# Moving start-up loads, position writes and scale rows between DMA queues, and one image's projections in the stage order, in a fused two-block convolution kernel

## The chip, the cores and the metric

The kernel runs on one core of a Trainium2 chip. Its time is the device time of one execution in microseconds (us); 18 executions of the kernel before were measured. One more thing about names: TensorE multiplies matrices (PE in the profile), VectorE (DVE) and ScalarE (ACT) work element by element, GpSimd (POOL) fills constants here and issues DMAs, SyncE (SP) only issues DMAs. Each engine runs its own instructions strictly in order, so a DMA that an engine issues also waits for what stands ahead of it on that engine.

## What is computed

Two bottleneck blocks, one after the other, on 16 images of 1024 channels and 32x32 pixels, all in float32. Cut to what matters, with `bn` a scale and a shift per channel:

```python
# block 0: 1x1 convolution to 256 channels, 3x3 self-attention, 1x1 convolution back
h = relu(bn(conv1x1(x, w_conv1)))
q, k, v = relu(bn(conv1x1(h, wq))), relu(bn(conv1x1(h, wk))), bn(conv1x1(h, wv))
logit[tap] = sum over 8 channels of a head of q * (k shifted by tap + pos[tap])   # 9 taps
a = relu(bn(sum over taps of softmax(logit)[tap] * (v shifted by tap)))
x = relu(bn(conv1x1(a, w_conv3)) + x)
# block 1: 1x1, 3x3 and 1x1 convolutions; inv = gamma / sqrt(var + eps)
y = relu(bn(conv1x1(x, w1)))
y = relu(bn(conv3x3(y, w2)))
x = relu(bn(conv1x1(y, w3)) + x)
```

## The kernel before, in words

**Stages.** The work on TensorE is a list of stages written out by hand (lines 933 to 938), one letter and an image number each. `C` is the first convolution of an image (`first_conv`: 8 chunks of 128 channels, each loaded as a 512 KB tile `x`), `Q` the projections to k, q and the position term, `V` the projection to v; `P` stands for C, Q and V in a row. `F` (`fused`) is the end of block 0 together with the first convolution of block 1, in 8 chunks that need `x` again as `s` and write their sum to DRAM as `r`. `W` (`winograd_conv`) is the 3x3 convolution for four images at once in Winograd form: 18 products, each with a transformed weight piece `U` and a transformed input piece `V__`. `U` (`last_sum`) is the last convolution: 8 chunks that load `r` back, seed the sum with it, and write to `out_dram`. A chunk of 8 matrix products takes 3.43 us.

**Side work.** The attention of an image (`logits`, `weighted`) and the Winograd transform of an image (`transform`, 22 us) run on VectorE beside the stages. The class `Side` keeps a model of both engines' time with fixed costs and decides by it in which order VectorE's steps are put into the program; the order is fixed when the program is built. `side.finish(b)` puts all of an image's attention ahead of its stage F.

**Buffers and queues.** `xpool` has 8 tiles; `more_loads` (line 304) issues the next load whenever a tile was given up, in the order of the list `loads`, from GpSimd (from ScalarE for image 0). `wpool` has 6 weight tiles, loaded from SyncE by `more_weights` in the order of use; a weight is loaded anew when its last use is more than 3 stages back. `zpool` has 3 tiles, shared by the softmax trees, the transforms, the Winograd sums and the scale rows. A transform writes its pieces to DRAM (`v<-v`, line 690) in three pairs of columns, (1, 2), (3, 4) and (0, 5); a `V__` load of part 0 or 1 reads columns of the first two pairs and a load of part 2 the last pair. In the kernel before, every `V__` load of four images stands behind all three pairs of the last image (`forms`, lines 310 and 694).

**DMA slots.** The compiled program shows that the DMAs issued by SyncE and ScalarE share 8 completion semaphores in turn, and those issued by GpSimd have 8 of their own: a DMA is issued only when the one eight places earlier, by the same group, has landed.

**Start.** `at_first` (line 1115) sets the order. ScalarE first takes the square root of the norms (line 151, behind a load of its function table), then issues four `x` tiles, three taps `g` (the 3x3 weights, 384 KB each, line 248), three `x`, three taps, the last `x`, and the last convolutions' weights (line 211, four tiles of 512 KB). SyncE loads the first convolution's weights in eight pieces (line 126), then `wqk` and `wv` (line 128), then the scale rows (`scale_rows`, line 221): 1024 scales of a norm stand in SBUF as 128 partitions x 8 and are written to DRAM transposed, `o p -> p o`, so each 4-byte element goes to its own address; the row is then read back to all partitions (line 223). VectorE works out the norms (lines 150 to 160) and the position table (183, 189), then transforms the 3x3 weights from the taps (`winograd_weights`, lines 259 to 281).

**In a stage Q.** `q` is written to DRAM from SyncE (line 490) to be read back in another layout by GpSimd (line 520). The position term (line 470) is copied by ScalarE out of PSUM into the place of q's first half (line 479), which therefore waits until that half of q has been written to DRAM; ScalarE then issues two writes `pos<-q` (line 484).

**At the end of a chunk.** `Expand.result` (line 396) adds the shift and clips on ScalarE (1.1 us for 128x1024) and stores the tile from GpSimd.

Of the kernel before, what the change touches and what calls it, by code (L numbers as in the profile page):

```python
# [8 lines left out]
F32 = mybir.dt.float32  # L9
AF = mybir.ActivationFunctionType  # L10
# [61 lines left out]
def sa_bottleneck_kernel(ctx: ExitStack, tc: tile.TileContext, x, w1t, wqkvt, w3t, u1t, u2t, u3t, params, out):  # L72
# [38 lines left out]
    def more_weights():  # L111

        if not queue:
            return
        key = name, of, half = queue.pop(0)
        t = wpool.tile([P, HW], F32, tag="w", name=f"{name}{half}_{of[0]}")
        src = source(name, half)
        n, k = src.shape[-1], 1
        for d in src.shape[1:-1]:
            k *= d  # L120
        view = t[:, : k * n].rearrange("p (c n) -> p c n", n=n)
        if len(src.shape) == 4:
            view = t.rearrange("p (m j o) -> p m j o", m=NW, j=2)
        if of[1] == 0 and name == "w1":
            for c in range(k):
                nc.sync.dma_start(view[:, c], src[:, c])
        else:
            nc.sync.dma_start(view, src)
        pieces[key] = view
# [17 lines left out]
    bn_a = const.tile([P, _NBN], F32, tag="bn_a", name="bn_a")  # L147
    bn_r = const.tile([P, _NBN], F32, tag="bn_r", name="bn_r")
    bn_t = const.tile([P, _NBN], F32, tag="bn_t", name="bn_t")
    nc.vector.tensor_scalar(bn_a, bn_block("L1_conv_v1"), EPS, None, ALU.add)  # L150
    nc.scalar.activation(bn_r, bn_a, AF.Sqrt)

    nc.vector.reciprocal(bn_t, bn_r)
    nc.vector.tensor_mul(bn_t, bn_t, bn_a)
    nc.vector.tensor_add(bn_t, bn_t, bn_r)
    nc.vector.tensor_scalar(bn_t, bn_t, 0.5, None, ALU.mult)
    nc.vector.reciprocal(bn_r, bn_t)
    nc.vector.tensor_mul(bn_inv, bn_r, bn_block("L1_conv_g1"))
    nc.vector.tensor_mul(bn_t, bn_inv, bn_block("L1_conv_m1"))
    nc.vector.tensor_sub(bn_sh, bn_block("L1_conv_b1"), bn_t)  # L160


    members = const.tile([P, G], F32, tag="members", name="members")
# [17 lines left out]
    for n in range(NW):  # L181
        for half, name in enumerate(("L0_conv_pos_h", "L0_conv_pos_w")):
            nc.vector.tensor_tensor(
                offsets[:, n, 2 * half : 2 * half + 2],
                col(name, 3 * n, 2),
                col(name, 3 * n + 2).to_broadcast([P, 2]),
                ALU.subtract,
            )
        nc.vector.tensor_tensor(
            pos[:, n],  # L190
            members.unsqueeze(2).to_broadcast([P, G, NPOS]),
            offsets[:, n].unsqueeze(1).to_broadcast([P, G, NPOS]),
            ALU.mult,
        )

# [9 lines left out]
    def load_scaled():  # L205

        rooms = vh.rearrange("p r w -> p (r w)"), hpool.tile([P, 2 * HW], F32, tag="h", name="scaled")
        for which, src in enumerate((w3t, u3t)):
            for half in range(2):
                at = rooms[which][:, half * HW :][:, :HW].rearrange("p (n o) -> p n o", n=NW)  # L210
                nc.scalar.dma_start(at, src.rearrange("(n p) o -> p n o", p=P)[:, :, halves(half)])
                scaled[which, half] = at

    def clear_hidden():
# [2 lines left out]
    def scale_rows():  # L217

        for which, scale in enumerate((col("L0_conv_bn3_s", 0, NC), bn_inv[:, 2 * NW : 2 * NW + NC])):
            row = dram.tile([NC, P], F32, tag=f"row{which}", name="row")  # L220
            nc.sync.dma_start(row.rearrange("o p -> p o"), scale)
            t = zpool.tile([P, HW], F32, tag="z", name="scales")
            nc.sync.dma_start(t, AP(row.tensor, row.offset, [[0, P], [1, C]]))
            scales.append(t)

    def scale_weights():

        for which in range(2):
            for half in range(2):
                t = scaled[which, half]  # L230
                nc.vector.tensor_tensor(
                    t, t, scales[which][:, halves(half)].unsqueeze(1).to_broadcast([P, NW, HALF]), ALU.mult
                )
                nc.sync.dma_start(ws[which, half], t)
                yield 1.3


# [3 lines left out]
    def load_taps(m):  # L241
        n = 3 * WID

        tag, shape = (("e", [P, KK, JPIX]), ("bnv", [P, HEAD_DIM, HALO]))[m]
        t = apool.tile(shape, F32, tag=tag, name="g").rearrange("p a b -> p (a b)")
        g = [t[:, i * n : (i + 1) * n] for i in range(3)]
        for i in range(3):
            nc.scalar.dma_start(g[i], u2t[m * P : (m + 1) * P, i * n : (i + 1) * n])
        taps.append(g)

    def winograd_weights():
# [53 lines left out]
    def more_loads():  # L305

        while credits[0] and loads:
            kind, b, c = loads[0]
            if kind == "V":
                if forms.get(b, 0) < NK:  # L310
                    return
                src = form_room(b)[c[0], c[1]].rearrange("p k j e -> p (k j e)")
            elif kind == "r":
                if (b, c) not in stored:
                    return
                src = stored[b, c]
# [5 lines left out]
            (nc.scalar if kind == "x" and b == 0 else nc.gpsimd).dma_start(t, src)  # L322
            loaded[loads.pop(0)] = t
            credits[0] -= 1
# [34 lines left out]
    class Expand:  # L359
# [28 lines left out]
        def result(self, o, to):  # L388
            t = self.tiles.pop(o)
            ps, to_ = self.ahead.pop(o), t  # L390

            if self.kind == "s":
                ps, to_ = ps.rearrange("p (n j) -> p j n", j=4), t.rearrange("p (j n) -> p j n", j=4)
            else:
                ps, to_ = ps.rearrange("p (j n) -> p n j", j=4), t.rearrange("p (n j) -> p n j", j=4)
            nc.scalar.activation(to_, ps, RELU, bias=self.shift(o), scale=1.0)  # L396
            nc.gpsimd.dma_start(to, t)  # L397
            return t
# [23 lines left out]
    def project(b):  # L422
# [42 lines left out]
        def positions():  # L465

            ps = psum.tile([P, HW], F32, tag="ps", name="ps")
            for half in range(2):
                for n in range(NW):
                    nc.tensor.matmul(  # L470
                        ps[n * G * NPOS : (n + 1) * G * NPOS, halves(half)],
                        pos[:, n].rearrange("p g t -> p (g t)"),
                        q[:, n, halves(half)],
                        start=True,
                        stop=True,
                    )

            by_offset = q[:, 0, :]
            nc.scalar.activation(by_offset, ps, AF.Identity)

            room, backs["pos"] = by_quarter("pos", b, JPIX, NPOS)
            by_offset = by_offset.rearrange("p (j w) -> p j w", j=NJ)
            for n in range(NW):
                nc.scalar.dma_start(room[n], by_offset[n * G * NPOS : (n + 1) * G * NPOS])

        k = halo("bnk", 1, RELU)
        yield next(k)
        for n in range(NW):
# [160 lines left out]
    def transform(b, src):  # L649
# [47 lines left out]
        more_loads()  # L697

    def winograd_conv(b):

# [215 lines left out]
    stages = []  # L916
    for text in (
# [4 lines left out]
    ):  # L922
# [190 lines left out]
    made = []  # L1113

    def at_first():
        credits[0] = 4
        more_loads()
        load_taps(0)
        credits[0] = 3
        more_loads()  # L1120
        load_taps(1)
        credits[0] = CHUNKS - 7
        more_loads()
        load_scaled()
# [4 lines left out]
        scale_rows()  # L1129
        hooks["conv1", 2, 0] = clear_hidden  # L1130

    at_first()
# [42 lines left out]
```

## Time and profile before

| | us |
|---|---|
| median of 18 executions | 2476.07 (2468.81 to 2482.71) |
| the profiled execution, its own time | 2475.61 |
| span of its instructions | 2473.7 |
| TensorE busy with products | 2399.3 |
| VectorE busy | 2076.6 |
| ScalarE busy | 918.2 |
| GpSimd busy | 411.0 |
| first product starts | 10.61 |
| last product ends | 2467.47 |
| data moved by DMA | 709.94 MB, 287 GB/s in the mean |

How to read it: "busy" counts the time in which an engine executes, and issuing a DMA counts for GpSimd alone. The time outside the span (1.9 us here) lies ahead of the first instruction and behind the last. A wait is listed with the event that ended it. The DMA queue q10 is ScalarE's, q1 is SyncE's and q0 is GpSimd's; all three run on the same 16 DMA engines. The granted clock of TensorE in a stretch is 1.00 at full speed.

### The profile page before, as it was taken

The numbers are of one execution on the slowest core, as the hardware profiler recorded it, in microseconds if no ns is written. First come the engines' busy times: TensorE is split into PE (matmuls) and PEld (weight loads), VectorE is DVE, ScalarE is ACT, GpSimd is POOL, SyncE is SP. The second block draws the span as 40 slices with busy tenths as digits, with TensorE's granted clock in tenths as the row PEclk, the third lists the DMA queues.
The fourth block names the chain that finished last, engine by engine and source line by source line (L and its number), as shares of the span: only waits on it lengthen the run. The fifth ranks groups of instructions, "written<-read, shape, count | busy, mean of one in ns | idle before, by whom it ended". The sixth has DMA issues, their size and how long they took to land.

```text
span 2473.7 us, 18390 instructions
## 1 busy us (share of the span) xinstructions
PE 2399.3 (97%) x6144; PEld 1157.1 (47%) x6144; DVE 2076.6 (84%) x1631; ACT 918.2 (37%) x873; POOL 411.0 (17%) x777
## 2 busy tenths in 40 slices
PE   5999999999999999999999999999999999998998
PEld 2444444444457443444457443444466444434843
DVE  2799998989989999998889999799989999964700
ACT  1423232242312574324222564324222553343275
POOL 1110101011111122111111122111111121112122
PEclk8999999999999999999999999999999999999999
DMA  8977787877888899788789899689788797789888
GB/s 257 352 260 268 251 286 241 268 238 266 304 288 267 306 332 330 264 295 298 247 263 322 306 310 349 237 296 314 259 306 300 275 354 251 280 307 306 300 248 279
DMA packets 328429, 709.94 MB, mean 287 GB/s; under 512 B 22672, under 2 KB 201872, under 8 KB 319632
## 3 DMA queue, kind: packets, MB, share of 16 engines
q0 software_dynamic: 110592, 441.24, 50.3%
q1 hardware_dynamic: 205792, 250.45, 31.3%
q10 hardware_dynamic: 11952, 17.09, 2.3%
q8 instruction: 49, 0.80, 0.1%
q14 instruction: 44, 0.36, 0.0%
HBM read 433.67 MB, written 275.03 MB: 286 GB/s over the span
## 4 chain that ended last, share of the span: by engine, by line
PE 73%; DMA 13%; issue 7%; DVE 4%; POOL 2%; ACT 1%; ACTq 0%; SPq 0%; POOLq 0%; DVEq 0%
PE ps L346 31%; PE ps L377 22%; PE ps L432 12%; PE ps L723 8%; DMA out_dram<-r 6%; DMA q<-q 1%; PE ps L470 1%; DMA row<-bn_inv 1%; DVE acc L590 1%; POOL r L322 1%; DVE acc L603 1%; DMA U<-uw 1%; DMA s<-in_x_dram 1%; DMA row<-par 1%; ACT h L975 1%
## 5 line engine op out<-in xcount | busy, mean ns | idle before, releaser
L377 PE MATMUL ps<-a,w 128*128 128x512 f32 x1024 | 464.9, 599 | 10.9 <-ACT ps L370 6.0
L346 PE MATMUL ps<-x,w 128*128 128x512 f32 x1024 | 449.9, 601 | 25.4 <-DMA x<-in_x_dram 25.4
L346 PE MATMUL ps<-s,u 128*128 128x512 f32 x1024 | 458.1, 593 | 1.0 <-ACT s L396 1.0
L377 PE MATMUL ps<-y,u 128*128 128x512 f32 x1024 | 442.4, 593 | 7.5 <-ACT ps L370 7.5
L539 DVE TENSOR_TENSOR prod<-qc,bnk 128x2048 f32<-128x2048 f32 x144 | 324.1, 2287 | 8.0 <-DMA a<-acc 6.3
L590 DVE TENSOR_TENSOR acc<-e,bnv 128x2048 f32<-128x2048 f32 x144 | 327.5, 2283 | 3.6
L346 PEld LDWEIGHTS ps<-x,w 128*128 128x128 f32 x1024 | 197.4, 193 | 274.7 <-issue 255.0
L377 PEld LDWEIGHTS ps<-a,w 128*128 128x128 f32 x1024 | 195.7, 192 | 262.4 <-issue 240.1
L396 ACT ACTIVATE s<-ps,par 128x1024 f32<-128x1024 f32 x128 | 142.4, 1113 | 464.5 <-PE ps L377 387.0
L377 PEld LDWEIGHTS ps<-y,u 128*128 128x128 f32 x1024 | 194.3, 190 | 253.6 <-issue 236.4
L346 PEld LDWEIGHTS ps<-s,u 128*128 128x128 f32 x1024 | 194.9, 190 | 245.8 <-issue 237.3
L603 DVE TENSOR_TENSOR acc<-acc 128x2048 f32<-128x2048 f32 x128 | 293.4, 2292 | 4.4
L432 PE MATMUL ps<-h,wqk 128*128 128x512 f32 x512 | 228.7, 602 | 8.5 <-ACT h L975 8.5
L397 POOL DMA_DIRECT2D r<-s x128 | 68.3, 533 | 730.2 <-ACT s L396 713.6
L396 ACT ACTIVATE r<-ps,bn_sh 128x1024 f32<-128x1024 f32 x128 | 141.8, 1108 | 110.5 <-PE ps L377 106.8
L544 DVE TENSOR_TENSOR prod<-prod 128x2048 f32<-128x2048 f32 (+1 forms) x80 | 166.2, 2077 | 2.3
L432 PEld LDWEIGHTS ps<-h,wqk 128*128 128x128 f32 x512 | 97.4, 192 | 137.3 <-issue 111.7
L370 ACT ACTIVATE ps<-r 128x1024 f32<-128x1024 f32 x128 | 130.3, 1020 | 50.9 <-DMA r<-r 37.9
L975 ACT ACTIVATE h<-ps,par 128x1024 f32<-128x1024 f32 x32 | 38.4, 1203 | 287.1 <-PE ps L346 287.1
L370 ACT ACTIVATE ps<-s 128x1024 f32<-128x1024 f32 x128 | 131.1, 1024 | 22.7 <-DMA s<-in_x_dram 19.0
L444 ACT ACTIVATE kp<-ps,par 128x1024 f32<-128x1024 f32 x64 | 77.2, 1207 | 133.6 <-PE ps L432 123.6
L322 POOL DMA_DIRECT2D s<-in_x_dram x128 | 67.8, 530 | 301.4 <-PE ps L346 186.8
(307 smaller groups left out, 2238.1 us busy)
## 6 DMA issues: line engine op xcount, KB each, us to landing
s<-in_x_dram POOLq DMA_DIRECT2D x128, 512.0 KB, 6.4
r<-s POOLq DMA_DIRECT2D x128, 512.0 KB, 4.9
r<-r POOLq DMA_DIRECT2D x128, 512.0 KB, 5.8
out_dram<-r POOLq DMA_DIRECT2D x128, 512.0 KB, 6.5
x<-in_x_dram POOLq DMA_DIRECT2D x120, 512.0 KB, 5.6
v<-v SPq DMA_DIRECT2D x96, 408.0 KB, 5.1
U<-uw SPq DMA_DIRECT2D x72, 512.0 KB, 7.3
bnk<-kp SPq DMA_DIRECT2D x32, 680.0 KB, 7.3
```

The lines of the kernel that those rows point to most:

```text
L322: (nc.scalar if kind == "x" and b == 0 else nc.gpsimd).dma_start(t, src)
L346: nc.tensor.matmul(ps[n][:, halves(half)], wt[:, c % (NC // 2), n * P : (n + 1) * P], src[:, halves(half)], start=(c == 0), stop=(c == NC ...
L370: nc.scalar.activation(ps, t, AF.Identity)
L377: nc.tensor.matmul(self.ahead[o][:, halves(half)], pieces[key][:, n, o % (NC // 2) * P :][:, :P], self.src[:, n, halves(half)], start=Fals ...
L396: nc.scalar.activation(to_, ps, RELU, bias=self.shift(o), scale=1.0)
L432: nc.tensor.matmul(ps[:, halves(half)], pieces[key][:, m, at : at + P], h[:, m, halves(half)], start=(m == 0), stop=(m == NW - 1),)
L444: nc.scalar.activation(dst, src, func, bias=col(f"L0_conv_{name}_b", n), scale=col(f"L0_conv_{name}_s", n),)
L539: nc.vector.tensor_tensor(by_row(t[:, two]), by_row(qc), kc[:, :, i : i + JROWS, j : j + W], ALU.mult)
L544: nc.vector.tensor_add(u[:, :, 0:4], u[:, :, 0:4], u[:, :, 4:8])
L590: nc.vector.tensor_tensor(by_row(dst), rows(e[:, k, :]).unsqueeze(1).to_broadcast([P, HEAD_DIM, JROWS, W]), vc[:, :, i : i + JROWS, j : j ...
L603: nc.vector.tensor_add(acc, acc, t)
L723: nc.tensor.matmul(acc[i][:, at, :, n, :], pieces[key][:, m, at, n * P : (n + 1) * P], v[:, at, :, m * (TILES + TR) :][:, :, :TILES], star ...
```

## The change

- At the start, ScalarE issues all eight `x` tiles of image 0 first; the square root and VectorE's norms come behind them (`norms()`), the position table later still (`position_table()`). Taps and last weights are issued by GpSimd. The first convolution's first weight half comes in two pieces (one channel block, then three) and the second half in one.
- The scale rows are written as they stand, 128 partitions x 8 elements (32 bytes in a row), and read back, by GpSimd; the multiplication of the last weights reads the scales in the new order (`p (m o) -> p o m`).
- `q` and the position term are written to DRAM by GpSimd. The position term is copied into a tile of `zpool` of its own.
- `V__` loads of parts 0 and 1 may be issued when the pairs (1, 2) and (3, 4) of the fourth image are on their way, those of part 2 when its pair (0, 5) is.
- The stage P10 moves from between F5 and F6 to behind F7, directly ahead of C11. P10 and C11, Q11 then share their `w1` and `wqk` loads.
- The very last output chunk is clipped in two halves, by ScalarE and VectorE, and stored in two halves by ScalarE's and SyncE's queues.

```diff
-            for c in range(k):
-                nc.sync.dma_start(view[:, c], src[:, c])
+            for part in (slice(0, 1), slice(1, k)) if half == 0 else (slice(0, k),):
+                nc.sync.dma_start(view[:, part], src[:, part])
...
-    nc.vector.tensor_scalar(bn_a, bn_block("L1_conv_v1"), EPS, None, ALU.add)
-    nc.scalar.activation(bn_r, bn_a, AF.Sqrt)
+    def norms():
+        nc.vector.tensor_scalar(bn_a, bn_block("L1_conv_v1"), EPS, None, ALU.add)
+        nc.scalar.activation(bn_r, bn_a, AF.Sqrt)
...
-                nc.scalar.dma_start(at, src.rearrange("(n p) o -> p n o", p=P)[:, :, halves(half)])
+                nc.gpsimd.dma_start(at, src.rearrange("(n p) o -> p n o", p=P)[:, :, halves(half)])
...
-            row = dram.tile([NC, P], F32, tag=f"row{which}", name="row")
-            nc.sync.dma_start(row.rearrange("o p -> p o"), scale)
+            row = dram.tile([P, NC], F32, tag=f"row{which}", name="row")
+            nc.gpsimd.dma_start(row, scale)
             t = zpool.tile([P, HW], F32, tag="z", name="scales")
-            nc.sync.dma_start(t, AP(row.tensor, row.offset, [[0, P], [1, C]]))
+            nc.gpsimd.dma_start(t, AP(row.tensor, row.offset, [[0, P], [1, C]]))
...
-            nc.scalar.dma_start(g[i], u2t[m * P : (m + 1) * P, i * n : (i + 1) * n])
+            nc.gpsimd.dma_start(g[i], u2t[m * P : (m + 1) * P, i * n : (i + 1) * n])
...
-                if forms.get(b, 0) < NK:
+                if forms.get((b, c[1] == 2), 0) < NK:
...
+            if (self.kind, self.b, o) == ("r", B - 1, NC - 1):
+                one, two = slice(0, JPIX // 2), slice(JPIX // 2, JPIX)
+                nc.scalar.activation(to_[:, one], ps[:, one], RELU, bias=self.shift(o), scale=1.0)
+                nc.vector.tensor_scalar(to_[:, two], ps[:, two], self.shift(o), 0.0, ALU.add, ALU.max)
+                nc.scalar.dma_start(to[:, :HALF], t[:, :HALF])
+                nc.sync.dma_start(to[:, HALF:], t[:, HALF:])
+                return t
...
-            by_offset = q[:, 0, :]
+            by_offset = zpool.tile([P, HW], F32, tag="z", name="by_offset")
...
-                nc.scalar.dma_start(room[n], by_offset[n * G * NPOS : (n + 1) * G * NPOS])
+                nc.gpsimd.dma_start(room[n], by_offset[n * G * NPOS : (n + 1) * G * NPOS])
...
-            nc.sync.dma_start(room[n], q[:, n, :].rearrange("p (j w) -> p j w", j=NJ))
+            nc.gpsimd.dma_start(room[n], q[:, n, :].rearrange("p (j w) -> p j w", j=NJ))
...
+            if two != (1, 2):
+                key = b - b % NK, two == (0, 5)
+                forms[key] = forms.get(key, 0) + 1
+                more_loads()
...
-        forms[b - b % NK] = forms.get(b - b % NK, 0) + 1
-        more_loads()
...
-        "F4 F5 P10 F6 F7 C11 Q11 W4 V11 C12 U4 Q12 V12 U5 U6 U7",
+        "F4 F5 F6 F7 P10 C11 Q11 W4 V11 C12 U4 Q12 V12 U5 U6 U7",
...
     def at_first():
-        credits[0] = 4
+        more_weights()
         more_loads()
-        load_taps(0)
-        credits[0] = 3
-        more_loads()
-        load_taps(1)
-        credits[0] = CHUNKS - 7
-        more_loads()
+        norms()
+        for m in range(NW):
+            load_taps(m)
         load_scaled()
-        for _ in range(4):
+        scale_rows()
+        for _ in range(3):
             more_weights()
+        position_table()
```

More of the change, by code (lines that the diff above doesn't have):

```diff
@@ L149, in sa_bottleneck_kernel @@
     bn_t = const.tile([P, _NBN], F32, tag="bn_t", name="bn_t")
-    nc.vector.tensor_scalar(bn_a, bn_block("L1_conv_v1"), EPS, None, ALU.add)
-    nc.scalar.activation(bn_r, bn_a, AF.Sqrt)
[L153 to L160, printed above, removed]
+    def norms():
+        nc.vector.tensor_scalar(bn_a, bn_block("L1_conv_v1"), EPS, None, ALU.add)
+        nc.scalar.activation(bn_r, bn_a, AF.Sqrt)
+        nc.vector.reciprocal(bn_t, bn_r)
+        nc.vector.tensor_mul(bn_t, bn_t, bn_a)
+        nc.vector.tensor_add(bn_t, bn_t, bn_r)
+        nc.vector.tensor_scalar(bn_t, bn_t, 0.5, None, ALU.mult)
+        nc.vector.reciprocal(bn_r, bn_t)
+        nc.vector.tensor_mul(bn_inv, bn_r, bn_block("L1_conv_g1"))
+        nc.vector.tensor_mul(bn_t, bn_inv, bn_block("L1_conv_m1"))
+        nc.vector.tensor_sub(bn_sh, bn_block("L1_conv_b1"), bn_t)
     members = const.tile([P, G], F32, tag="members", name="members")
@@ L180, in sa_bottleneck_kernel, with position_table @@
     pos = const.tile([P, NW, G, NPOS], F32, tag="pos", name="pos")
-    for n in range(NW):
-        for half, name in enumerate(("L0_conv_pos_h", "L0_conv_pos_w")):
+    def position_table():
+        for n in range(NW):
+            for half, name in enumerate(("L0_conv_pos_h", "L0_conv_pos_w")):
+                nc.vector.tensor_tensor(
+                    offsets[:, n, 2 * half : 2 * half + 2],
+                    col(name, 3 * n, 2),
+                    col(name, 3 * n + 2).to_broadcast([P, 2]),
+                    ALU.subtract,
+                )
             nc.vector.tensor_tensor(
[L184 to L187, printed above, removed]
-            )
[L189 to L194, printed above, removed]
+                pos[:, n],
+                members.unsqueeze(2).to_broadcast([P, G, NPOS]),
+                offsets[:, n].unsqueeze(1).to_broadcast([P, G, NPOS]),
+                ALU.mult,
+            )
     kp = const.tile([P, NW, H + 2, PW], F32, tag="kp", name="kp")
@@ L228, in scale_weights @@
         for which in range(2):
+            scale = scales[which].rearrange("p (m o) -> p o m", o=NC)
+            shape = [P, NW, NC // 2, P]
             for half in range(2):
-                t = scaled[which, half]
+                t = scaled[which, half].rearrange("p n (o m) -> p n o m", m=P)
                 nc.vector.tensor_tensor(
-                    t, t, scales[which][:, halves(half)].unsqueeze(1).to_broadcast([P, NW, HALF]), ALU.mult
+                    t, t, scale[:, half * NC // 2 :][:, : NC // 2].unsqueeze(1).to_broadcast(shape), ALU.mult
                 )
-                nc.sync.dma_start(ws[which, half], t)
+                nc.sync.dma_start(ws[which, half], scaled[which, half])
                 yield 1.3
@@ L1115, in at_first @@
     def at_first():
-        credits[0] = 4
+        more_weights()
         more_loads()
-        load_taps(0)
-        credits[0] = 3
-        more_loads()
-        load_taps(1)
-        credits[0] = CHUNKS - 7
-        more_loads()
+        norms()
+        for m in range(NW):
+            load_taps(m)
         load_scaled()
-        for _ in range(4):
+        scale_rows()
+        for _ in range(3):
             more_weights()
+        position_table()
         side.first(winograd_weights(), 24.0, 0.0)
         side.first(scale_weights(), 24.0, 0.0)
-        scale_rows()
         hooks["conv1", 2, 0] = clear_hidden
```

## The prediction, as put on record

> **What bounds the kernel now.** I read the shares of busy time first, then the list of what TensorE waited for, then the timeline of TensorE at those places, and the chain that ended last only to see what stood behind them.
>
> ```profile
> PE 2399.3 (97%) x6144; PEld 1157.1 (47%) x6144; DVE 2076.6 (84%) x1631; ACT 918.2 (37%) x873; POOL 411.0 (17%) x777
> ```
>
> TensorE is the bound: 2399 of 2474 us. Nothing here removes a product, so a gain can only come from the 74 us in which TensorE stands still and from products at a slow clock. Where these are:
>
> ```profile
> PE ps L346 <- DMA x<-in_x_dram: 25.4, 3, 10.6
> PE ps L377 <- ACT ps L370: 13.4, 10, 4.1
> PE ps L432 <- ACT h L975: 8.5, 13, 3.3
> PE ps L723 <- issue: 7.3, 2, 6.2
> PE ps L377 <- ACT a L629: 4.9, 2, 2.5
> PE ps L723 <- DMA U<-uw: 4.0, 1, 4.0
> PE ps L723 <- ACT z L746: 3.1, 1, 3.1
> ```
>
> (Total us, times, longest.) The largest is the load of image 0. TensorE's timeline there (start, length, idle before):
>
> ```profile
> 10.61 16.47 PE L346 MATMUL ps<-x,w 128*128 128x512 f32 x32 [10.61 <-DMA x<-in_x_dram]
> 35.35 12.60 PE L346 MATMUL ps<-x,w 128*128 128x512 f32 x24 [8.27 <-DMA x<-in_x_dram]
> 54.50 6.41 PE L346 MATMUL ps<-x,w 128*128 128x512 f32 x8 [6.55 <-DMA x<-in_x_dram]
> 64.17 6.26 PE L432 MATMUL ps<-h,wqk 128*128 128x512 f32 x7 [3.26 <-ACT h L975]
> ```
>
> The first convolution's 64 products end at 60.9; in the second image the same 64 take 27.5 us (89.9 to 117.4). Besides the gaps, products run at half speed after each: 32 take 16.47 us where 13.74 is usual.
>
> Why x comes so late: the chain and the stretches of DMA.
>
> ```profile
> 5.69 14.79 DMA row<-par
> 20.94 20.79 DMA row<-bn_inv
> ```
>
> ```profile
> 14.00:20.00 6.00, 6.00 (x13) 2.58 (x12) 0.00 (x0) 0.00 (x0) 0.68 (x1) 1.00 0.62 44
> 22.00:32.00 10.00, 5.08 (x12) 1.90 (x10) 0.96 (x1) 0.00 (x0) 1.06 (x2) 0.86 1.08 400
> 32.00:38.00 6.00, 2.65 (x3) 1.17 (x4) 0.00 (x0) 0.00 (x0) 0.00 (x0) 0.50 0.72 52
> ```
>
> The last three columns are granted clock, DMA share and GB/s. While either scale row is written in 4-byte pieces (from 5.69 and from 20.94), all DMA falls to 44 and 52 GB/s; between them it is 400. As DMAs of SyncE and ScalarE share eight slots in turn, ScalarE's taps and later x tiles also wait for these rows to land: the fifth x is issued at 21.15, the last at 48.62.
>
> **The change, part by part.**
>
> *Opening.* x now stands behind `par` alone, which takes ScalarE's queue from 0.81 to 1.23. The first x took 7.0 us from issue (3.58) to first product (10.61); so 8.2, and I take 8.5 as taps now load beside it. Then 2.7 us of slow clock and 27.5: 38.7, and 0.9 for small gaps between x tiles: 39.6, where Q starts now at 64.17. Q and V of image 1 take 23.4 us (117.4 to 140.8), those of image 0 took 25.7 (64.17 to 89.9) with a cold clock, which goes with the gaps. So image 1's convolution starts at 63.0 and not at 89.9: **26.9 less**.
>
> Cover: x must arrive at 3.43 us per 512 KB, 153 GB/s. In 22 to 32 us ScalarE's queue moved 1.72 MB beside 1.75 of GpSimd's and 0.53 of SyncE's:
>
> ```profile
> q0 software_dynamic: 476, 1.75, 48.6%
> q10 hardware_dynamic: 584, 1.72, 42.7%
> q1 hardware_dynamic: 840, 0.53, 16.7%
> ```
>
> 172 GB/s is 3.05 us per tile. In 2 to 14 it was 139 GB/s, 3.8 us: then the eighth x lands at 8.5 + 7 x 3.8 = 35.1, just when TensorE asks for it (8.5 + 2.7 + 7 x 3.43 = 35.2). What is late next is VectorE, whose 3x3 weights began in earnest at 51.97. Now: GpSimd's memset of `kp` ends at 3.40, three taps (1.18 MB at 139 GB/s, 8.5 us, plus about 2.5 of latency as `par` shows) land near 15; the norms wait for ScalarE to issue all x (the last waits for the slot of an early DMA, about 12.5), then table load 1.28, norms 2.2 and positions 0.9: near 17. So about 18, 33 us earlier, more than TensorE's 27. ScalarE's weight work ahead of `h` took 11.8 us (51.10 to 62.93): done at 30, before 38.7.
>
> The new scale row, 128 pieces of 32 bytes: not in the trace. Ends: 14.79 us as the old one, nothing; nearest is `par` (128 pieces, issued 0.81, used 3.36), 2.5 us, which I take. It stands on GpSimd ahead of image 1's x; these now go out near 25 and are needed at 63, so even 14.8 twice would cost little. The multiplication with strided scales: 4 x 1.22 us; twice that is hidden, as VectorE is 6 us ahead.
>
> *q and position term.* ScalarE's copy waits for q's write 26.5 us in eight cases (ACT q L479 from DMA q<-q). With its own tile that wait is gone. What TensorE lost by it: 0.30 + 1.00 + 0.35 at 501 to 511, **1.6**; and at W4:
>
> ```profile
> 1269.73 3.69 PE L723 MATMUL ps<-V__0_4355,U 128*128 128x256 f32 x16 [1.09 <-issue]
> 1280.01 3.72 PE L723 MATMUL ps<-V__1_4359,U 128*128 128x256 f32 x16 [3.14 <-ACT z L746]
> ```
>
> ScalarE stood 8.39 us before its copy at 1276.42, and the sums `z` behind it came late; the first gap is the late `V__`, whose transform ran up to 1262. P10 in between gives 51 us more for it. **4.2 less.** F6 then comes 51 us sooner, at 952 + 112 - 27 = 1037, and F7 at 1092; attention 6 ended at 951 and 7 at 1071, less 27 and with 16 us of relay 940 and 1060, in time. The added wait: the copy needs the `zpool` tile of three uses back. Closest is image 8, copied at 714, where VectorE had filled that tile by 692 and its store takes 5.1. ScalarE's sums stand behind the copy, and VectorE may wait about 1 us for the tile three uses on.
>
> GpSimd gains 64 + 14 DMAs. Those of q have 512 pieces instead of 128: between 0.53 (its price for any size now) and 4 x 0.53 each; I take 0.53. In stage Q GpSimd has issued the next x already, so it is idle there; from F and U stages on I charge **2 more** in all.
>
> *W0:* 4.0 from a late U. The listing of the compiled order leaves its issue behind the second `bnk` write, so it moves little: **1 less** (0 to 4).
>
> *W12:* gap 6.20 at 2281.78.
>
> ```profile
> 2273.65 0.53 POOL L397 DMA_DIRECT2D out_dram<-r  x1 [2.95 <-ACT r L396]
> 2274.33 0.53 POOL L322 DMA_DIRECT2D V__0_8020<-v  x1 [0.16 <-issue]
> ```
>
> The load stands behind the eighth output store; in the new order behind the fifth (2263.30). Then its data decide: the third column store is issued at 2263.83, 5.1 to land, load 7.4: 2276.3 instead of 2281.8. I take **5 less**.
>
> *Last chunk:* ScalarE 1.11 us, issue, landing; last product at 2467.47, end 2473.75. Half the clip saves 0.5 (VectorE's 128x512 from PSUM is 0.68); a half store from the other queues is not shown, 0 to 2.9 less. **1 less.**
>
> *Unchanged:* 4.3 at 933 to 962, 7.4 at 1481 to 1514 (output stages, DMA share 0.87 to 1.05), 4.9 at 2183 (attention 15).
>
> Sum: -26.9 -1.6 -4.2 +2 -1 -5 -1 = -37.7 on the profiled 2475.6, which lies 0.5 below the median: 2437.9, **2438 us**.
>
> **The rivals.**
>
> 1. *x starves behind taps and weights*, 4.4 MB on GpSimd that used to come later. If x gets a third of the 288 GB/s of 2 to 14, a tile takes 5.4 us, the eighth lands at 46.3 and Q starts at 49.7; with a cold clock image 1 starts at 75.4, 14.5 less, and 2475.6 - 14.5 - 10.8 = **2450**. Against: SyncE's 1.8 MB are soon done. The Trainium skill (DMA: Bandwidth & Descriptors, section Queues, rings and completion order) says that each DMA engine goes round the queues that have work; by that rule three busy queues get such thirds, and the 1.75 and 1.72 MB above agree with even shares of two. Chance 0.15.
> 2. *The later gaps come back elsewhere*, as output stages are full of DMA and VectorE is 84% busy: only opening and end remain, 2475.6 - 26.9 - 1 + 2 = **2450**. Chance 0.22.
> 3. *The unchanged gaps close as well* (16.6, half of it taken, and all of W0's): 2438 - 8.3 - 3 = **2427**. Chance 0.1.
> 4. *Slower: GpSimd's queue becomes the bound.* It issues nearly all x, s, r and the outputs; every us it stands still in F or U is lost once the eight tiles (27 us) run dry. If the 512-piece writes cost 4 x 0.53, four an image are 6.3 us more, 101 us in 16 images, and without slack 2438 + 101 = **2539**. From 2.7 us an image on ((2481 - 2438) / 16) it is slower than before. Against: GpSimd is busy 17%, and its issues take 527 to 534 ns beside a VectorE that is 84% busy. The Trainium skill (SBUF — State Buffer, section SBUF: two separate sides) warns that VectorE's two-port operations lock GpSimd out of writing descriptors, which would stretch the moved issues; those 527 to 534 ns show no such lock. Chance 0.03.
>
> The forecast itself: 0.5. About 0.2% is what a measurement can tell. Faster by more: the forecast and rivals 1 to 3, less 0.02 for a milder form of rival 4 on top of them that ends the same: 0.95; same 0.02; slower 0.03. Range: rivals 1 to 3 are inside, with the ends for the opening (20 to 30 less), the stores and W0: 2422 to 2456.
>
> **What would show it.** First product near 8.5, no gap over 1 us in the first convolution, Q of image 0 near 40, image 1 near 63; DMA above 250 GB/s throughout the first 40 us; no wait of ScalarE for q<-q; no gaps at W4; the gap at W12 under 1.5. Wrong it would be if x tiles come at more than 4 us, or GpSimd shows long issues of q, or output stages wait more than 12 us in all.

## The result, and the profile after

| | before | after |
|---|---|---|
| median, us | 2475.33 (48 executions) | 2441.65 (8, 2438.11 to 2443.5) |
| profiled execution, us | 2475.61 | 2439.14 |
| span of its instructions | 2473.7 | 2437.0 |
| TensorE idle (gaps over 0.15 us), summed | 67.9 | 41.0 |

The ratio is 0.9864, with a 95% interval of 0.9854 to 0.9875: the change is faster by 1.4%. The prediction was 2438 us; of the 38 us that it forecast 33.7 came.

The page of the profile after, busy time by engine:

```profile
PE 2390.9 (98%) x6144; PEld 1153.8 (47%) x6144; DVE 2080.9 (85%) x1632; ACT 918.2 (38%) x873; POOL 464.9 (19%) x854
```

TensorE has lost 8 us of busy time without losing a product: fewer gaps leave fewer products at half speed. GpSimd (POOL) has gained 54 us. What TensorE waited for (total us, times, longest):

```profile
PE ps L385 <- ACT ps L378: 12.6, 8, 4.4
PE ps L448 <- ACT h L992: 11.1, 13, 5.9
PE ps L354 <- DMA x<-in_x_dram: 6.4, 1, 6.4
PE ps L740 <- DMA V__1_2433<-v: 4.4, 1, 4.4
PE ps L385 <- ACT a L644: 2.7, 1, 2.7
```

The wait for `x` has fallen from 25.4 us to the 6.4 before the first product, W12's 6.2 and W4's 3.1 are gone, the seeds of the output stages (`ps L378`, line 370 before) stay. The 4.4 put down to a load of `V__` was another wait (*W0* below). And one wait for `h` has grown to 5.9. TensorE's timeline at the start and at that place (start, length, idle before):

```profile
6.38 29.40 PE L354 MATMUL ps<-x,w 128*128 128x512 f32 x64 [6.38 <-DMA x<-in_x_dram]
35.61 1.02 PE L448 MATMUL ps<-h,wqk 128*128 128x512 f32 x2
...
52.95 1.93 PE L486 MATMUL ps<-q,pos 128*64 128x512 f32 x6 [1.74 <-ACT q L460]
...
61.78 4.46 PE L354 MATMUL ps<-x,w 128*128 128x512 f32 x10
```

```profile
138.80 1.45 PE L354 MATMUL ps<-x,w 128*128 128x512 f32 x3
146.10 14.07 PE L448 MATMUL ps<-h,wqk 128*128 128x512 f32 x28 [5.85 <-ACT h L992]
```

Image 0's 64 products run through without a gap, and image 1 starts at 61.8 instead of 89.9: 28.1 us less. At image 2's projections 5.85 us are lost again, and image 3's first convolution starts at 170.7 instead of 191.6: 20.9 less. ScalarE's timeline shows the cause:

```profile
142.83 2.12 ACT L586 ACTIVATE e<-e 128x2304 f32<-128x2304 f32 x1 [20.85 <-DVE e L583]
144.86 2.28 ACT L992 ACTIVATE h<-ps,par 128x1024 f32<-128x1024 f32 x2
```

Image 0's exponential stands ahead of image 2's `h` on ScalarE and waits 20.85 us for VectorE, whose attention began late: it comes behind the 3x3 weights, and their last step starts at 85.7 (104.4 before), only 18.7 us sooner, although they began in earnest at 21.4 instead of 52.0. Behind them stands the multiplication of the last weights, here with the scales in strided order (`vh` and `scaled`, two each; before, line 231, one took 1220 ns):

```profile
L238 DVE TENSOR_TENSOR scaled<-scaled,scales 128x1024 f32<-128x1024 f32 x2 | 3.9, 2012 | 0.0
```

Its four steps cost 3.2 us more than before, so the exponential starts at 142.8 instead of 158.3, only 15.5 sooner. Why the 3x3 weights are slow is shown by VectorE's waits between 20 and 100 us and by the stretches of the whole kernel (the last three columns are granted clock, DMA share and GB/s):

```profile
DVE u L270 <- DMA uw<-u: 18.2, 5, 7.1
```

```profile
14.00:20.00 6.00, 6.00 (x15) 2.66 (x14) 0.97 (x6) 2.67 (x4) 0.56 (x1) 1.00 1.02 400
20.00:32.00 12.00, 12.00 (x29) 5.33 (x28) 11.02 (x27) 4.21 (x11) 1.09 (x2) 1.00 0.92 349
32.00:38.00 6.00, 5.56 (x13) 2.20 (x12) 3.81 (x11) 4.41 (x9) 0.69 (x2) 1.00 0.96 298
38.00:60.00 22.00, 20.26 (x49) 8.19 (x48) 11.87 (x23) 11.11 (x19) 6.85 (x12) 1.00 1.03 382
60.00:94.00 34.00, 33.56 (x79) 14.76 (x78) 21.69 (x40) 13.04 (x27) 5.82 (x11) 1.00 1.04 370
```

The collapses to 44 and 52 GB/s are gone, but now DMA is full from 14 to 94 us (share 0.92 to 1.04). VectorE makes a 768 KB piece of weights every 2.65 us when nothing holds it (27.63, 30.28 and 32.93), 297 GB/s, and waits 18.2 us for tiles whose stores have not landed, the longest time (7.1, up to 51.2) while image 1's `x` are loading.

How far ahead the kernel after is at later places (the two traces' starts subtracted): F0 20.9 us, F2 22.7, W0 23.4, the end of W0 22.9, F4 18.4, W4 20.0, its end 23.4, F8 23.0, W8 23.8, the end of F15 28.1, W12 34.5, the last product 35.3, the end 36.7.

### The profile page after: what moved, and what is told of

Read it like the earlier page. It is cut to its first block, busy times and chain, and to the rows that moved or that the text cites. A ratio compares the mean times of both kernels' runs of the same rounds, so it can differ in the third digit from the quotient of the medians.

```text
span 2437.0 us, 18415 instructions
## 1 busy us (share of the span) xinstructions
PE 2390.9 (98%) x6144; PEld 1153.8 (47%) x6144; DVE 2080.9 (85%) x1632; ACT 918.2 (38%) x873; POOL 464.9 (19%) x854
## 4 chain that ended last, share of the span: by engine, by line
PE 58%; DVE 26%; DMA 10%; issue 3%; ACT 1%; POOL 1%; SPq 0%; ACTq 0%; DVEq 0%; POOLq 0%
PE ps L385 23%; PE ps L354 22%; PE ps L740 8%; PE ps L448 6%; DVE acc L605 5%; DVE acc L618 5%; DVE prod L554 4%; DMA out_dram<-r 3%; DVE prod L559 2%; DMA uw<-u 2%; DVE v L669 1%; DVE form L669 1%; DMA v<-v 1%; DVE prod L560 1%; DMA bnk<-kp 1%
## 5 line engine op out<-in xcount | busy, mean ns | idle before, releaser
L354 PE MATMUL ps<-x,w 128*128 128x512 f32 x1024 | 443.9, 594 | 6.4 <-DMA x<-in_x_dram 6.4
L448 PE MATMUL ps<-h,wqk 128*128 128x512 f32 x512 | 227.4, 599 | 11.1 <-ACT h L992 11.1
L378 ACT ACTIVATE ps<-r 128x1024 f32<-128x1024 f32 x128 | 130.4, 1021 | 55.0 <-DMA r<-r 47.5
L378 ACT ACTIVATE ps<-s 128x1024 f32<-128x1024 f32 x128 | 131.2, 1025 | 17.8 <-DMA s<-in_x_dram 15.3
L330 POOL DMA_DIRECT2D r<-r x128 | 68.2, 533 | 299.7 <-DMA out_dram<-r 187.1
```

The costliest lines, as they stand in the source:

```text
L354: nc.tensor.matmul(ps[n][:, halves(half)], wt[:, c % (NC // 2), n * P : (n + 1) * P], src[:, halves(half)], start=(c == 0), stop=(c == NC ...
L378: nc.scalar.activation(ps, t, AF.Identity)
L448: nc.tensor.matmul(ps[:, halves(half)], pieces[key][:, m, at : at + P], h[:, m, halves(half)], start=(m == 0), stop=(m == NW - 1),)
```

## The experiments

The experiments ran on two chips on which the kernel before took 2467 to 2469 us, so ratios to the kernel before beside them are compared, and places in the traces. The changed kernel itself, the exponential alone, the old queues and the last combination ran beside each other on one of them, the other eight on the other. There is one trace of the kernel before, taken with the result's measurement and not on these chips. So places compared with it carry a difference of several us: the run of the later edits, which keeps the old opening, has F0 5.4 us sooner than that trace.

**The opening alone.** The kernel before with the diff's hunks for weights, norms, taps, scale rows and `at_first`, and none of the others.

> The kernel before with the edits of the opening alone (x ahead of the norms and taps, taps, last weights and contiguous scale rows on GpSimd's queue); q, positions, image 10, the counts of forms and the last chunk stay as before. Theory of the prediction: all of what the opening gains up to image 1 is kept, 26.9 us, so 2475.3 - 26.9 = about 2448 us. Rival, read from the trace of the changed kernel: 28 us are gained up to image 1's convolution, and 7 of them are lost again when image 0's exponential stands ahead of image 2's h on ScalarE, so about 21 are kept: 2454 us, with a wait of TensorE of 5 to 6 us for h of image 2 near 146 us.

Measured: 2446.76 us, ratio 0.992 (0.990 to 0.9939), about 20 us of 2469 (15 to 25). So not all of the 26.9 us was kept, as the rival says. In its trace image 1 starts at 62.0 and F0 at 219.8, 22.6 sooner than in the trace before; 5.2 us were lost at image 2, in gaps of 1.30 and 2.24 (for `h`, where the rival has 5 to 6) and the half-speed products behind them.

**The later edits alone.** The other hunks, and the old opening.

> The kernel before with all edits but those of the opening: q and positions by GpSimd with a tile of their own, image 10 behind F7, forms counted by columns, last chunk in halves. Theory of the prediction: its terms 1.6 + 4.2 + 1 + 5 + 1 - 2 = 10.8 less, 2464.5 us. Rival, read from the trace: the later edits carry what the opening lost, 36.7 - 20.9 = 15.8 less, 2459.5 us. If both parts interact (later stages only gain because everything is earlier against VectorE), less than 8: over 2467 us.

Measured: 2456.28 us, ratio 0.9955 (0.9939 to 0.997), 11 us: the prediction's 10.8. That they agree is in part luck: by its trace W4 (with the 1.09 us ahead of it) brings 4.6 us and the way from F15 to W12 6.4, but from W0's end to F4's end 11.4 are lost, which no term has. The two halves give 0.8 + 0.45 = 1.25%; the whole change gave 1.36% in the result, 1.3% on the second chip. They add up, within their intervals.

**Only the scale rows written by partition.**

```diff
-            row = dram.tile([NC, P], F32, tag=f"row{which}", name="row")
-            nc.sync.dma_start(row.rearrange("o p -> p o"), scale)
+            row = dram.tile([P, NC], F32, tag=f"row{which}", name="row")
+            nc.sync.dma_start(row, scale)
```

(and `scale_weights` as in the change). All queues and orders are those of before.

> The kernel before with one edit: the two scale rows are written by partition in 128 pieces of 32 bytes instead of 1024 of 4, on the same queue of SyncE and at the same place; x, taps and last weights stay on ScalarE's queue in the old order. Theory: the 4-byte writes held the slots and the DMA engines, so DMA stays near 400 GB/s from 5 to 40 us, TensorE's wait for x falls from 25.4 us to under 10 and the time to about 2460 us. Rival: the order on ScalarE's queue (taps between the x tiles) sets x's landing; the wait for x stays over 15 us, time over 2466 us.

Measured: 2457.03 us, ratio 0.9955 (0.994 to 0.997), 11 us. By the traces F0 starts at 225.9, 16.5 sooner than before, and 11.1 sooner than in the run of the later edits (237.0), which has the old opening on the same chip. TensorE's waits and start:

```profile
PE ps L349 <- DMA x<-in_x_dram: 12.0, 2, 9.5
```

```profile
9.46 27.36 PE L349 MATMUL ps<-x,w 128*128 128x512 f32 x56 [9.46 <-DMA x<-in_x_dram]
39.38 5.40 PE L349 MATMUL ps<-x,w 128*128 128x512 f32 x8 [2.56 <-DMA x<-in_x_dram]
48.78 15.88 PE L435 MATMUL ps<-h,wqk 128*128 128x512 f32 x32 [4.00 <-ACT h L978]
```

Between the two theories: the first convolution's gaps fall from 25.4 to 12.0 us with the taps still between the `x`, and DMA holds 237 to 402 GB/s from 14 to 38 us, although the first row still took 11.0 us to land (5.55 to 16.59). Image 1 starts at 73.4, 11.6 later than after the whole change; yet the last step of the 3x3 weights starts at 87.2 against 85.7, and F0 comes only 4.4 later: here TensorE loses nothing at image 2, where the whole change loses 7.2. By time this one edit gives about half of what the opening gives, 11 of some 20 us.

**The scattered rows again, in the changed kernel.** The same two lines, the other way round, on GpSimd's queue.

> The changed kernel with the two scale rows written in 1024 pieces of 4 bytes again, on GpSimd's queue behind taps and last weights. Theory: the pieces slow all DMA wherever they come from: while they are written, DMA falls under 100 GB/s for 15 to 20 us each and the x of image 0 that still miss, or image 1's x, come late: TensorE loses 10 to 20 us before 100 us, ratio 0.990 to 0.994. Rival: only the shared slots of SyncE and ScalarE made them dear; on GpSimd's queue they delay nothing but image 1's x, which has time: ratio under 0.988.

Measured: 2439.86 us, ratio 0.9889 (0.9866 to 0.9911), where the changed kernel has 0.987 on the other chip and 0.9864 in the result: 2 to 6 us more, with intervals that overlap and hold a part of each theory's range. So the trace must tell. The stretch of 30 to 38 us:

```profile
30.00:38.00 8.00, 7.56 (x19) 3.14 (x18) 4.01 (x11) 4.46 (x8) 0.00 (x0) 1.00 1.22 41
```

The theory is right in its mechanism and wrong in its price: DMA falls to 41 GB/s from GpSimd's queue too, but by then `x` of image 0 has landed (28.7). Image 1 starts at 67.5, 5.7 later than after, and F0 at 224.0, 2.5 later. Where the pieces stand in the order decides what they cost.

**Image 0's exponential behind image 2's `h`, first try.** The plan's time for it was put 13 us later, which moves it behind both `h` and leaves VectorE's order as it is.

```diff
-                self.exp = self.vector, cost
-                if job["b"] == 0:
-
-                    self.fire()
+                self.exp = self.vector + (13.0 if job["b"] == 0 else 0.0), cost
```

> The changed kernel with one thing moved: on ScalarE image 0's exponential stands behind both h of image 2 and not ahead of them (its planned time 13 us later; VectorE's order is the same). Theory: the 5.85 us wait for h at 146 us was this order alone, it goes and nothing takes its place: 2441.7 - 5.9 = about 2436 us. Rival: VectorE's late end of the 3x3 weights is what counts, attention 0 sets F0 anyway and TensorE waits there instead: 2441 us, a new wait at 215 to 225 us.

Measured: 2485.11 us, ratio 1.0073 (1.0053 to 1.0093), slower than the kernel before. The wait at 146 us is gone (image 3 starts at 164.9), but the plan's clock for VectorE stays 13 us late, and the order of the other engines follows it: ScalarE's relu of the first attended image, landed at 208.7, stands behind other work until 221.25 (TensorE waits 6.65 at F0), and W8 shows gaps of 14.87 and 11.93. Neither theory is told by this run; it moved more than one thing.

**The same, alone.** The plan's time is put back once the exponential is placed.

```diff
-            self.jobs[0]["at"] = max(at, self.tensor) + EXP
+            self.jobs[0]["at"] = (max(at, self.tensor) if self.jobs[0]["b"] else at - 13.0) + EXP
```

> The changed kernel, image 0's exponential behind both h of image 2 on ScalarE as in the run with the exponential moved, but with the planned times put back afterwards, so that the order of ScalarE, SyncE and VectorE is otherwise that of the changed kernel (on GpSimd two loads of x stand ahead of image 1's relays). Theory: that run lost because the later planned times also moved ScalarE's relu of the attended image behind V of image 3; alone, the move takes the 5.85 us wait at 146 us away, attention 0 is there 9 us before F0 asks for it, so 5 to 6 us less than the changed kernel: ratio to before about 0.984. Rival: VectorE sets the following stages, the 5.85 us come back as waits up to 500 us: ratio 0.986 to 0.987.

Measured: 2435.27 us, ratio 0.9872 (0.985 to 0.9894), the rival's and not the theory's. It was run once more beside the changed kernel, below.

**The position copy in q's tile again.**

```diff
-            by_offset = zpool.tile([P, HW], F32, tag="z", name="by_offset")
+            by_offset = q[:, 0, :]
```

> The changed kernel with the position product's copy put back into q's tile (the writes stay on GpSimd's queue). Theory of the prediction: ScalarE waits again for q's write, the 1.6 us at about 480 to 490 us come back and some of the 4.2 us at W4: 2 to 5 us more than the changed kernel, ratio 0.987 to 0.9885. Rival: the queue mattered and not the tile, ScalarE's waits fall into time that it has: ratio 0.986 to 0.987, no new gap of TensorE.

Measured: 2440.49 us, ratio 0.9891 (0.9871 to 0.9912): by time it can't be told from the changed kernel. In its trace ScalarE waits 33.3 us for q's write in seven cases (26.5 in eight before), and TensorE has no gap over 0.7 us between 145 and 697 us: the 1.6 us at 501 to 511 did not come back. The runs of the opening alone and of the rows alone, with q's old tile and old queue, have only 0.4 us there too. So these 1.6 us do not need the edits of q; what took them away is not settled. But right behind, in W0, ScalarE's copy and then TensorE stand:

```profile
695.90 1.02 ACT L494 ACTIVATE q<-ps 128x1024 f32<-128x1024 f32 x1 [10.16 <-DMA q<-q]
```

```profile
697.89 5.25 PE L740 MATMUL ps<-V__1_2321,U 128*128 128x256 f32 x16 [4.43 <-ACT z L763]
```

There the wait for q's write does cost TensorE, 4.4 us.

**Image 10 at its old place, in the changed kernel.**

```diff
-        "F4 F5 F6 F7 P10 C11 Q11 W4 V11 C12 U4 Q12 V12 U5 U6 U7",
+        "F4 F5 P10 F6 F7 C11 Q11 W4 V11 C12 U4 Q12 V12 U5 U6 U7",
```

> The changed kernel with image 10's projections back between F5 and F6. Theory of the prediction: W4's waits come back, 4.2 us (late V__ and late sums z): 2445 to 2447 us, ratio 0.988. Rival: these gaps came from ScalarE's copy that waited for q's write, and that is gone with the tile of its own: no gap over 1 us at W4, ratio 0.986 to 0.987.

Measured: 2457.41 us, ratio 0.9955 (0.994 to 0.997): some 20 us more than the changed kernel on the other chip, far over the forecast's 4.2. GpSimd's timeline, and ScalarE's at W4:

```profile
1238.76 0.53 POOL L330 DMA_DIRECT2D V__1_4342<-v  x1
1249.72 0.53 POOL L330 DMA_DIRECT2D V__2_4362<-v  x1 [10.43 <-DMA v<-v]
...
1251.80 1.53 POOL L505 DMA_DIRECT2D q<-q  x2
1253.32 1.26 POOL L499 DMA_DIRECT2D pos<-by_offset  x2
```

```profile
1243.94 1.03 ACT L494 ACTIVATE by_offset<-ps 128x1024 f32<-128x1024 f32 x1 [0.66 <-PE ps L486]
...
1270.64 1.02 ACT L763 ACTIVATE z<-ps 128x1024 f32<-128x1024 f32 x1 [18.45 <-DMA pos<-by_offset]
```

The load of `V__2` waits on GpSimd for the last transform's columns; q's and the positions' writes are queued behind it; the positions' are issued 8.3 us after the copy was done, land another 16.6 us later, at 1270.5, and the third `z` of W4 needs their tile of `zpool`. TensorE stands 13.68 us, and W4 is 16.6 us longer than after (78.9 and 62.3). So moving the writes to GpSimd's queue made a new wait at W4, and moving image 10 took it away: the two edits belong together.

**The changed kernel again, beside the next three.**

> The changed kernel itself, on the chip of this group, so that the other three have it beside them: ratio to before 0.986 as in the result, 2440 to 2442 us.

Measured: 2437.41 us, ratio 0.987 (0.9855 to 0.9884).

**The exponential alone, beside it.**

> The version with only image 0's exponential moved behind h of image 2, beside the changed kernel on one chip. Theory: the 5.85 us wait goes and stays away: 5 to 6 us under the changed kernel. Rival: what it gains up to 500 us is given back by other waits in the rest: within 2 us of it.

Measured: 2438.47 us, ratio 0.9874 (0.9856 to 0.9893), the same as the changed kernel within some 5 us. The wait for `h` at this place, 3.9 us in the run beside it, is gone, and F0 starts 5.4 us sooner than in the run beside it (215.9 and 221.3), F2 0.4 later. The gain is gone within one stage F:

```profile
322.49 7.03 PE L385 MATMUL ps<-a,w 128*128 128x512 f32 x16
332.61 5.40 PE L354 MATMUL ps<-s,u 128*128 128x512 f32 x8 [3.08 <-ACT s L412]
```

A gap of 3.08 us in F1 that the changed kernel has not, and products at half speed behind it: eight take 5.40 us where 3.60 is usual. The rival was right: what is gained at 146 us is given back by F2. Why `s` is late there was not tested.

**q and positions back on SyncE's and ScalarE's queues.**

```diff
-                nc.gpsimd.dma_start(room[n], by_offset[n * G * NPOS : (n + 1) * G * NPOS])
+                nc.scalar.dma_start(room[n], by_offset[n * G * NPOS : (n + 1) * G * NPOS])
...
-            nc.gpsimd.dma_start(room[n], q[:, n, :].rearrange("p (j w) -> p j w", j=NJ))
+            nc.sync.dma_start(room[n], q[:, n, :].rearrange("p (j w) -> p j w", j=NJ))
```

> The changed kernel with q's writes back on SyncE's queue and the position product's on ScalarE's; the tile of its own stays. Theory of the prediction: 64 issues on GpSimd cost about 2 us in all, so 0 to 2 us less than the changed kernel. Rival: on SyncE and ScalarE the writes wait for one of the eight shared slots and the engines stand behind them: 2 to 6 us more, with waits of ScalarE or of h, kp, q behind its DMA issues.

Measured: 2432.17 us, ratio 0.9848 (0.9831 to 0.9866): the fastest of all runs, 5.2 us under the changed kernel beside it (the intervals overlap a little; all four executions lie under all four of it). VectorE's waits between 20 and 100 us:

```profile
DVE u L270 <- DMA uw<-u: 8.6, 3, 6.7
```

8.6 us, where the run beside it has 16.7 and the result's trace 18.2: the last step of the 3x3 weights starts at 78.8 against 84.3, the exponential comes at 136.0, ahead of the end of image 2's convolution, its `h` waits for nothing, and F0 starts at 213.9 against 221.3. Of this lead of 7.4 us 3.6 is left at the end of the span. That the stores land sooner is shown, by which way the two queues bring it about is not.

**Both: image 10 at its old place and the old queues.**

> Image 10 back between F5 and F6 and q and positions back on SyncE's and ScalarE's queues, all else as in the changed kernel. In the run with image 10 alone at its old place, GpSimd held at a load of V__ that waited for the last image's columns to be stored (1239.3 to 1249.7 us), q's and the positions' writes stood behind it, and ScalarE waited 18.45 us for the position tile: 13.7 us at W4. Theory: that queue order is the cause; with the writes on other queues ScalarE's wait falls under 8 us and W4's gap under 5 us: 8 to 12 us less than that run (2457 us there), 2445 to 2449 us. Rival: the writes land late because DMA is full there, whichever queue: the gap at W4 stays over 10 us.

Measured: 2438.0 us, ratio 0.9877 (0.986 to 0.9893). W4:

```profile
1257.20 5.03 PE L740 MATMUL ps<-V__2_4362,U 128*128 128x256 f32 x11 [3.74 <-DMA U<-uw]
```

A gap of 3.74 us instead of 13.68, and ScalarE's third `z` waits 2.43 for TensorE alone. On ScalarE's queue the positions' writes land 6.0 and 6.7 us after issue, not 16.6: the place on GpSimd's queue was the cause. With the old queues the move of image 10 is worth 2438.0 - 2432.2 = 5.8 us, near the forecast's 4.2; with the writes on GpSimd it is worth some 20.

## Why the prediction came out as it did

The time was right to 0.15%, in part by luck. The working was right in its parts up to image 1 and in W4 and W12; some terms were mis-sized, some reasons did not hold, and the errors cancelled.

*Opening.* First product at 6.38 (8.5 predicted), Q of image 0 at 35.6 (39.6), image 1 at 61.8 (63.0): 28.1 less, 26.9 predicted. The last `x` landed at 29.25 where 35.1 was expected, so there was no gap behind the first product. The step that failed is the cover: "VectorE is 6 us ahead". It did begin early (21.4, about 18 predicted, as ScalarE's last `x` was issued at 16.84 and not at 12.5; the third tap was there at 13.9, 15 predicted) but waited 18.2 us for its stores, which the sum had not counted, and the strided multiplication, hidden in the sum, took 3.2 us more. Of the 33 us that VectorE was to be earlier, 15.5 are left at the exponential; TensorE came there 28.1 earlier, had to wait, and is 20.9 ahead at F0. The run of the opening alone shows a loss at the same place, that of the old queues shows it gone with shorter waits for stores.

*The new row.* 2.5 us was taken, from `par`. It took 16.3 us from issue to landing (14.22 to 30.51), as the waits of GpSimd show:

```profile
POOL scales L227 <- DMA row<-par: 16.0, 1, 16.0
```

The size of the row was not it: the second, of the same size, took 5.7 us with less ahead of it on the queue. Of the 4.4 MB of taps and weights issued before the first, 3.1 were still to move. The prediction also took a scattered row to hold DMA from its issue on; but the stretch at 400 GB/s (22 to 32) lies inside the second row's 20.94 to 41.72, so it does so for a part of that time only. The bound "14.79 twice costs little" held in kind: image 1's `x` went out at 37.8 and not at 25, landed from 45 to 58, and was needed from 61.8.

*q and position term.* F0 to F2 brings 1.7 (1.6 predicted), but the gap also stays away without the tile of its own and nearly so with q's old tile and queue, so the reason given is not shown. W4 took 62.3 us instead of 65.6, and the 1.09 ahead of it are gone: 4.5 less (4.2). The added wait for the tile was put at "about 1 us" for VectorE. It fell on ScalarE, 9.2 us at W0 (and 18.45 at W4 in the run without the move of image 10). GpSimd's queue was charged 2 us; the run with the old queues says about 5, at the edge of the noise. One issue of q takes 764 to 778 ns, not 527, and one of the positions 632; but the price lies in what stands ahead of the write, not in its issue.

*W0.* 1 less was predicted; its length went from 69.7 to 70.2 us. The late U is gone, but a gap of 4.41 is there again:

```profile
705.86 1.02 ACT L763 ACTIVATE z<-ps 128x1024 f32<-128x1024 f32 x1 [9.18 <-DMA pos<-by_offset]
```

```profile
706.93 6.67 PE L740 MATMUL ps<-V__2_2345,U 128*128 128x256 f32 x16 [4.41 <-DMA V__1_2433<-v]
```

The load named there can't have ended it: it landed at 708.40, and its tile is first used at 723.8. TensorE goes on 0.05 us after ScalarE's third `z`, and in four other runs the profile names `z` for the same product. So this is the wait for the positions' tile, priced at about 1 us: 4.4 us, and 16 products behind it at half speed (6.67 us, 3.62 is usual). In the second trace of the changed kernel ScalarE waits 4.5 us, TensorE 0.3, and W0 takes 63.1.

*W12.* 6.4 less between F15 and W12's start (5 predicted). The 6.20 us gap is gone in every run with the new count of columns (1.9 at most) and there in both runs without it (5.94 and 6.70).

*Last chunk.* 6.27 to 4.75 us behind the last product, 1.5 less (1 predicted). The reason was half wrong: VectorE's half of the clip starts when ScalarE's is done (2432.30 to 2432.99, 2433.02 to 2433.77), so together they take 1.47 where the whole took 1.11. The gain lies behind: in these two traces a half store lands 2.0 to 2.1 us after its issue, the whole one took 2.9. Ten of the eleven traces with halves show 4.5 to 5.1, the eleventh 8.86; the three without show 6.26 to 6.97.

*"Unchanged".* The output stages U1 to U3 grew from 4.3 to 7.0 us of gaps, 4.5 us of lead; from W8 to the end of F15 4.3 us came in, all in F15, whose wait for attention 15 fell from 4.9 to 2.7. These two cancel, which is luck. All output stages together wait 12.6 us, over the 12 that the prediction gave as a sign of being wrong.

*Rivals.* Rival 1: `x` did not starve. A tile came every 3.3 us beside the taps. By that rival its queue was to get a third; from 2 to 14 us it moved 1.98 of 4.44 MB, 45%, so equal thirds of the bytes is not what this trace shows. Rival 2 was half right: the opening is where later waits took back most. Rival 3 did not come: of its 16.6 us 15.3 are left, with U1 to U3 worse and F15 better. Rival 4: a mechanism like it exists (a write late behind what stands ahead on GpSimd's queue), in W stages and not in every image; at W4 the stage order hides it (some 20 us without), at W0 it cost 4.4. The lock of which the Trainium skill warns (SBUF — State Buffer, section SBUF: two separate sides) does not show: the 32 issues of q lie within 14 ns of each other beside a VectorE that is 85% busy. But all save 30 us of VectorE's time is in TENSOR_TENSOR (1699 us) and SCALAR_TENSOR_TENSOR (397 us), and no trace here shows whether any of them is of the two-port kind, so the warning is not tested.

## What to carry to other kernels

When a start-up gap is closed, follow the gain to the next engine that must deliver: here image 1 started 28 us sooner and the first later meeting with VectorE left 21 of them, and one edit (rows in one piece per partition) gave about half of what the opening gave. Before a write is moved to another queue, list what stands ahead of it there and what that waits for; a load that waits for data holds everything behind it, and a short issue time says nothing of this. Two edits that look independent can be a damage and its repair, so test each with the other undone: the version without the move of q's and the positions' writes is the fastest here, by 5 us at the edge of the noise. And before a wait is explained by the event that the profile names, look whether that event came before the engine went on.

## What the runs showed of the hardware that was not expected

- A row of 1024 pieces of 4 bytes takes all DMA with it from either queue tried, for 6 to 8 us: 41 GB/s from GpSimd's, 44 and 52 from SyncE's before.
- A write of 4 KB took 16.3 us with 3.1 MB still ahead of it on its own queue and 5.7 us with less; the positions' writes took 16.6 us behind four loads on GpSimd's queue and 6.0 to 6.7 on ScalarE's. In these cases the place and not the size set when a DMA landed.
- A 128x1024 float32 multiplication on VectorE took 2.01 us with one input read in steps of 32 bytes, 1.22 with that input in a row.
- The same kernel before took 2475 us on one chip and 2467 to 2469 on two others; small differences are only to be read between runs on one chip.
